# Layer 1 of a four-layer transformer on one core: FFN products issued ahead of the gates, SiLU written as a sigmoid, gate products on GpSimd, norms and copies on two engines

## The chip, the cores and the metric

The kernel runs on 1 core of a Trainium2 chip. A core has five engines that run side by side, each with an instruction queue of its own, in order: TensorE (PE; its weight loads are shown apart as PEld), VectorE (DVE), ScalarE (ACT), GpSimd (POOL) and SyncE (SP), which here issues nearly all ordinary DMAs. Data lies in SBUF (128 partitions); matmul results go to PSUM, which has 8 banks of 128 x 512 floats here. Engines wait for each other by semaphores. The metric is device time in microseconds; lower is better. All data is float32.

## What is computed

A stream `x` of 4 x 512 tokens of 128 features passes four layers. Each layer is a half-weighted FFN, an attention (or a recurrence) and the same FFN again, each on a normalised copy of `x`:

```python
x = x + 0.5 * ffn(layernorm(x));  x = x + attn(layernorm(x));  x = x + 0.5 * ffn(layernorm(x))
```

The layers that matter here are 1 and 2. The FFN of layer 1 has 8 experts of width 64 and a shared expert of width 128. Each token is given the two experts with the largest scores:

```python
shared = (silu(x @ ws_gate.T) * (x @ ws_up.T)) @ ws_down.T
scores = sigmoid(x @ gate_weight.T)              # 8 per token
topk_w, topk_idx = top_k(scores, 2)
topk_w = topk_w / (sum(topk_w) + 1e-20) * 2.5    # combine: these, on the two experts, else 0
hmid = silu(x @ w_gate.T) * (x @ w_up.T)         # per expert, 64 wide
out = sum_over_experts(combine * (hmid @ w_down.T)) + shared
```

`silu(g)` is `g * sigmoid(g)`. The FFN of layer 2 has no nonlinearity between its two matrices, so the kernel multiplies them beforehand into one 128 x 128 matrix per expert; its two gates are a softmax over two scores, worked out as sigmoids of their difference. The "attention" of layer 2 is a gate, `sigmoid(a) * silu(b)`, a scan along the sequence with decay 0.9, and an output matrix. Layers 0 and 3 have causal attention of 16 heads and FFNs that send tokens to experts.

## The kernel before, in words

**Tiling.** The stream stays in SBUF as four tiles `xs[b]` (b = 0 to 3), each 512 tokens as 4 blocks of 128 rows by 128 features. Layers 1 and 2 work on *pairs*: the first pair is b = 0, 1, the second b = 2, 3. The code is written as Python generators; `skewed` (L1437) runs one part of each in turn, with the second pair some rounds behind: 5 rounds in the first FFN of layer 1 (L1504) and 8 in the long chain (L1536).

**Order.** The order of each engine's instructions is set by the framework's planner, which goes by the written order and by its own estimate of when inputs are ready. In the attentions the order of PE, DVE, ACT and POOL is as written (L804). In the long chain, POOL's order alone is as written (L1535).

**Stages.** In order of time: layer 0; `prep_l2` (L1214), the products of layer 2's matrices, beside the end of layer 0's second FFN; the first FFN of layer 1 (`l1_ffn`, L1075); layer 1's attention (`l1_attn`, L1143); then the chain (`behind`, L1508), which is for each pair: layer 1's second FFN, layer 2's FFN (`l2_ffn`, L1254), its recurrence (`l2_attn`, L1323), its second FFN, and the sending of tokens to layer 3's experts (L408, indirect DMAs on POOL); then layer 3.

**A norm.** `norms` (L152): DVE works out mean and variance of each block of 128 tokens (L160, L161); POOL makes `rs`, `rstd` and `off` for all blocks (L164 to L169); then each block is scaled by rstd and shifted, by the engine that the caller names (L171 to L178). `normed_T` (L1039) asks for ACT, turns the blocks on PE (`T_f`, L187) and copies them out of PSUM on ACT (`nT`, L1046). It has five callers' runs per pair: `l1_ffn` twice, `l2_ffn` twice, `l2_attn` once.

**The FFN of layer 1.** The scores are matmuls of 8 columns (`scored`, L1051), then a sigmoid on ACT (L1081). The gates are 16 small DVE instructions (`route` twice, `without`, L1083 to L1094). They are turned on PE (`gT`, L1068), copied by ACT (L1070), written to DRAM and read back spread over 64 partitions per expert (`cb`, L1102), on SP's queue. Then, for each b of the pair, five steps: the shared expert first (k = 0), then two experts at a time (k = 1 to 4). A step is

```python
nc.tensor.matmul(ps[0], gw, nTs[x], start=True, stop=True)     # L1127
nc.tensor.matmul(ps[1], uw, nTs[x], start=True, stop=True)     # L1128
nc.scalar.activation(h, ps[0], AF.Silu)                        # L1130
nc.vector.tensor_tensor(h, h, ps[1], ALU.mult)                 # L1131
nc.vector.tensor_tensor(h, h, cbs[x][:, c, :], ALU.mult)       # L1133, k > 0 only
```

and two steps later its down product (L1115, accumulated in one PSUM bank). At the end of each b the bank is added to `xs[b]` (L1140). `h` has 6 buffers.

**Other names.** `copy` (L131) takes DVE and ACT in turn, by a count over the whole program. In `prep_l2`, for each of 8 experts, PE turns one matrix, ACT copies it (L1246), PE multiplies (L1249), and ACT copies the result into `m` (L1252). L1267 and L1269 are the sigmoids of layer 2's gates, L1333 and L1335 those of the recurrence.

Of the kernel before, what the change touches and what calls it, by code (L numbers as in the profile page):

```python
# [9 lines left out]
FP = mybir.dt.float32  # L10
I32 = mybir.dt.int32
AF = mybir.ActivationFunctionType
ALU = mybir.AluOpType
# [28 lines left out]
def kernel(ctx: ExitStack, tc: tile.TileContext, a: dict, out: bass.AP):  # L42
# [109 lines left out]
    def norms(srcs, dsts, tag, on="vector", fine=False):  # L152

        g = len(srcs) * NT
        st = small.tile([P, g, 6], FP, name=f"st_{tag}", tag=f"bn_st{g}")
        mv = small.tile([P, g, 2], FP, name=f"mv_{tag}", tag=f"bn_mv{g}")
        rs = small.tile([P, g], FP, name=f"rs_{tag}", tag=f"bn_rs{g}")
        rstd = small.tile([P, g], FP, name=f"rstd_{tag}", tag=f"bn_rstd{g}")
        for t in range(g):
            nc.vector.bn_stats(st[:, t, :], srcs[t // NT][:, t % NT, :])  # L160
            nc.vector.bn_aggr(mv[:, t, :], st[:, t, :])  # L161
            if fine and t % 2 and t < g - 1:
                yield
        nc.gpsimd.tensor_scalar(rs, mv[:, :, 1], EPS, None, ALU.add)  # L164
        nc.gpsimd.tensor_tensor(rstd, rs, mhalf[:, :g], ALU.pow)
        if on != "vector":
            off = small.tile([P, g], FP, name=f"off_{tag}", tag=f"bn_off{g}")
            nc.gpsimd.tensor_scalar(off, mv[:, :, 0], -1.0, None, ALU.mult)
            nc.gpsimd.tensor_tensor(off, off, rstd, ALU.mult)  # L169
        yield  # L170
        for t in range(g):  # L171
            src, dst = srcs[t // NT][:, t % NT, :], dsts[t // NT][:, t % NT, :]
            if on == "scalar":
                nc.scalar.activation(dst, src, AF.Identity, bias=off[:, t : t + 1], scale=rstd[:, t : t + 1])
# [864 lines left out]
    def normed_T(pool, bs, tag):  # L1039

        ns = [work.tile([P, NT, D], FP, name=f"n{b}_{tag}", tag="n", bufs=3) for b in bs]
        yield from norms([xs[b] for b in bs], ns, tag, "scalar")
        nTs = []
        for n, b in zip(ns, bs):
            nT = work.tile([P, S], FP, name=f"nT{b}_{tag}", tag="nT", bufs=4)
            nc.scalar.copy(nT, transposed(n, f"{b}_{tag}"))  # L1046
            nTs.append(nT)
        yield
        return nTs
# [25 lines left out]
    def l1_ffn(pool, i, bs):  # L1075
        tag = f"f1{i}_{bs[0]}"
        G = len(bs) * NT
        nTs = yield from normed_T(pool, bs, tag)
        plg = scored(nTs, l1["gate"], tag)
        sc = pool.tile([P, G, E], FP, name=f"sc_{tag}", tag="sc1")  # L1080
        nc.scalar.activation(sc, plg, AF.Sigmoid)  # L1081
# [12 lines left out]
        nc.vector.tensor_tensor(comb, comb, bc(total, [P, G, E]), ALU.mult)  # L1094
        yield
        cbs = []
        for x, b in enumerate(bs):
            rows = to_rows(pool, comb, x, f"{b}_{tag}")

            cb = pool.tile([P, NC, S], FP, name=f"cb{b}_{tag}", tag="spread", bufs=4)  # L1100
            for u in range(2):
                nc.sync.dma_start(  # L1102
                    cb[u * I1 : (u + 1) * I1],
                    bass.AP(tensor=rows.tensor, offset=rows.offset + u * S, ap=[[0, I1], [2 * S, NC], [1, S]]),
                )
            cbs.append(cb)
        order = [NC] + list(range(NC))
        for x, b in enumerate(bs):
            po = bank(f"o{b}_{tag}").rearrange("p (t d) -> p t d", d=D)
            hs = []  # L1110

            def down(k):

                for t in range(NT):
                    nc.tensor.matmul(  # L1115
                        po[:, t, :],
                        hs[k][:, t * P : (t + 1) * P],
                        l1["down"][order[k]],
                        start=(k == 0 and t == 0),
                        stop=(k == NC and t == NT - 1),  # L1120
                    )

            for k, c in enumerate(order):
                gw = l1["wg"][:, c * P : (c + 1) * P] if c < NC else l1["sg"]
                uw = l1["wu"][:, c * P : (c + 1) * P] if c < NC else l1["su"]
                ps = pair(f"gu{c}_{b}_{tag}")
                nc.tensor.matmul(ps[0], gw, nTs[x], start=True, stop=True)  # L1127
                nc.tensor.matmul(ps[1], uw, nTs[x], start=True, stop=True)  # L1128
                h = pool.tile([P, S], FP, name=f"h{c}_{b}_{tag}", tag="h1", bufs=6)
                nc.scalar.activation(h, ps[0], AF.Silu)  # L1130
                nc.vector.tensor_tensor(h, h, ps[1], ALU.mult)  # L1131
                if c < NC:
                    nc.vector.tensor_tensor(h, h, cbs[x][:, c, :], ALU.mult)  # L1133
                hs.append(h)
# [79 lines left out]
    def prep_l2(pool):  # L1214
# [25 lines left out]
        for e in range(E):  # L1240
# [2 lines left out]
            for c in range(NC):  # L1243
                nc.tensor.transpose(ps[:, c * P : (c + 1) * P], wo[:, c * P : (c + 1) * P], ident)
            woT = pool.tile([P, FF], FP, name=f"wo2T_{e}", tag="woT", bufs=3)
            nc.scalar.copy(woT, ps)  # L1246
            pm = bank(f"m2_{e}")
            for c in range(NC):
                nc.tensor.matmul(  # L1249
                    pm[:, :D], wi[:, c, :], woT[:, c * P : (c + 1) * P], start=(c == 0), stop=(c == NC - 1)  # L1250
                )
            nc.scalar.copy(m[:, e, :], pm[:, :D])  # L1252

    def l2_ffn(pool, i, bs):  # L1254
        tag = f"f2{i}_{bs[0]}"
# [326 lines left out]
```

## Time and profile before

| | us |
|---|---|
| median of 9 runs | 1517.73 (1515.79 to 1520.4) |
| the profiled execution | 1517.43 |
| its span | 1515.5 |
| PE, DVE, ACT, POOL busy | 1266.8, 852.1, 713.1, 654.2 |
| `prep_l2`'s products | about 414 to 438 of the span |
| first FFN of layer 1, from its scores to the last down product | 438.6 to 505.9 |
| layer 1's attention | about 506 to 748 |
| the chain | about 748 to 1012 |

The span is the time from the first to the last instruction of the profiled execution, and stretches are given in microseconds from its start. In a timeline line stand start and length, the engine, the line of the code, the operation, `output<-inputs`, shapes, and in brackets how long the engine had been idle before and what ended that ("issue" where the profile shows nothing). Names are shortened: `h_f`, `cb_f`, `gT_f`, `n_f` are tiles of FFNs, with `_a` those of attentions and of the recurrence. A matmul in float32 is shown as two passes, so the "x" counts of PE are twice those of the code. The granted clock is the share of full speed that the throttle gave to TensorE.

### The profile page before, as it was taken

To read this page: it belongs to the slowest core of one execution; us is meant where nothing else is said; L and a number is where in the kernel's file an instruction comes from. 1 tells how busy PE (TensorE), PEld (TensorE's weight loads), DVE (VectorE), ACT (ScalarE), POOL (GpSimd) and SP (SyncE) were. 2 spreads that over 40 slices of the span, in tenths; PEclk is the share of its full clock that TensorE was granted. 3 is DMA by queue.
4 is the path that set the end of the run, shared out by engine and by line. 5 is a ranking of instruction groups with operands and counts; after the bars stand their busy time and mean duration, and the time that the engine had idled before them with its cause. 6 is when DMAs were issued, how large, how long until landed. Compare 5 with 4: busy or idle time off the path is not lost. (4 is left out here: it accounts for less than half of the span.)

```text
span 1515.5 us, 28724 instructions
## 1 busy us (share of the span) xinstructions
PE 1266.8 (84%) x10645; PEld 812.9 (54%) x10645; DVE 852.1 (56%) x2832; ACT 713.1 (47%) x1487; POOL 654.2 (43%) x776
## 2 busy tenths in 40 slices
PE   4788999996969689999799878729689999998394
PEld 3465666764746366667666656527433333342272
DVE  5226777663335367857556545534377787773342
ACT  1235877871453266867643232103336555564041
POOL 4356768761510287868401111544630234203253
PEclk9898999996999799999999868759889999999597
DMA  8420240002424575331050000032104000000233
GB/s 251 114 58 15 79 173 9 9 18 76 141 59 87 151 232 161 106 120 58 2 107 7 1 0 1 29 85 77 58 20 169 15 11 5 15 2 15 78 85 104
DMA packets 100659, 106.20 MB, mean 70 GB/s; under 512 B 9084, under 2 KB 73832, under 8 KB 100520
## 3 DMA queue, kind: packets, MB, share of 16 engines
q1 hardware_dynamic: 93864, 91.16, 21.0%
q0 software_dynamic: 6656, 13.22, 2.7%
q8 instruction: 84, 1.38, 0.4%
q14 instruction: 55, 0.45, 0.1%
HBM read 62.49 MB, written 41.85 MB: 69 GB/s over the span
## 5 line engine op out<-in xcount | busy, mean ns | idle before, releaser
L632 POOL TENSOR_SCALAR sc_a<-sc_a,top_a 128x128 f32<-128x128 f32 (+3 forms) x256 | 274.9, 1090 | 78.2 <-DVE top_a L617 51.7
L600 PE MATMUL s_a<-k_a,q_a 32*128 32x512 f32 (+3 forms) x1536 | 262.3, 546 | 20.6 <-DMA k_a<-fac_a 13.9
L709 ACT ACTIVATE w_a<-t_a 128x512 f32<-128x512 f32 x256 | 140.1, 595 | 117.2 <-PE t_a L600 89.2
L645 PE MATMUL t_a<-ident,sc_a 128*128 128x128 f32 x1280 | 171.6, 280 | 6.6 <-DVE top_a L621 6.0
L502 POOL DMA_INDIRECT res_f<-y_f,back_f x112 | 110.1, 983 | 134.7 <-ACT y_f L501 101.4
L600 PE MATMUL t_a<-ql_a,k_a 32*128 32x512 f32 x512 | 167.2, 647 | 0.3 <-DVE low_a__12648 L689 0.2
L645 PEld LDWEIGHTS t_a<-ident,sc_a 128*128 128x128 f32 x1280 | 142.5, 143 | 43.2 <-issue 16.1
L634 ACT ACTIVATE sc_a<-sc_a,top_a 128x128 f32<-128x128 f32 (+3 forms) x256 | 135.3, 576 | 28.0 <-DVE top_a L621 27.5
L600 PEld LDWEIGHTS s_a<-k_a,q_a 32*128 32x128 f32 x1536 | 90.8, 187 | 92.1 <-issue 40.3
L654 ACT ACTIVATE w_a<-t_a 128x256 f32<-128x256 f32 (+2 forms) x192 | 94.1, 526 | 67.1 <-PE t_a L645 66.7
L408 POOL DMA_INDIRECT disp_f<-n_f,to_f x96 | 95.1, 990 | 54.8 <-issue 36.7
L514 PE MATMUL o_f<-w_l,h_f 128*128 128x128 f32 (+1 forms) x896 | 113.2, 279 | 3.8 <-DVE o_f L496 3.3
L514 PEld LDWEIGHTS o_f<-w_l,h_f 128*128 128x128 f32 (+1 forms) x896 | 103.1, 184 | 15.0 <-DVE o_f L496 6.0
L479 PE MATMUL h_f<-dT_f,w_l 128*128 128x320 f32 (+1 forms) x256 | 105.6, 549 | 2.8 <-ACT dT_f L457 2.8
L164 POOL TENSOR_SCALAR rs_f<-mv_f 128x4 f32<-128x4 f32 (+1 forms) x23 | 5.8, 250 | 221.2 <-DVE mv_f L161 220.8
L667 PE MATMUL acc_a<-w_a,vpad 128*32 128x128 f32 x2560 | 97.3, 278 | 0.6 <-ACT w_a L654 0.6
L689 DVE TENSOR_REDUCE low_a__12648<-s_a 128x1 f32<-128x512 f32 x128 | 82.0, 684 | 27.8 <-PE t_a L600 20.0
L656 ACT COPY w_a<-t_a 128x256 f32<-128x256 f32 (+2 forms) x192 | 93.5, 526 | 6.2 <-PE t_a L645 6.1
L689 DVE TENSOR_REDUCE low_a__12646<-s_a 128x1 f32<-128x512 f32 x128 | 81.3, 683 | 18.4 <-PE t_a L600 12.5
L621 DVE CUSTOM_DVE_ANT_0 sc_a<-s_a,future 128x128 f32<-128x128 f32 (+3 forms) x128 | 62.3, 486 | 48.8 <-PE s_a L600 40.9
L501 ACT ACTIVATE y_f<-o_f,d_f 128x128 f32<-128x128 f32 (+1 forms) x112 | 38.8, 394 | 106.2 <-DVE o_f L496 102.6
L621 DVE CUSTOM_DVE_ANT_0 sc_a<-s_a,table 128x128 f32<-128x128 f32 (+3 forms) x128 | 62.3, 487 | 42.1 <-PE s_a L600 38.0
(343 smaller groups left out, 2253.7 us busy)
## 6 DMA issues: line engine op xcount, KB each, us to landing
fac_a<-fac_a_sb SPq DMA_DIRECT2D x36, 256.0 KB
disp_f<-zeros_f SPq DMA_DIRECT2D x4, 2080.0 KB
d_f<-disp_f SPq DMA_DIRECT2D x32, 260.0 KB
w_l<-in_L_ffn_w_dram SPq DMA_DIRECT2D x16, 512.0 KB
cb_f<-rows_f SPq DMA_DIRECT2D x16, 512.0 KB
q_a<-fac_a SPq DMA_DIRECT2D x32, 256.0 KB
k_a<-fac_a SPq DMA_DIRECT2D x32, 256.0 KB
r_f<-res_f SPq DMA_DIRECT2D x24, 256.0 KB
```

What stands on the lines that cost most here:

```text
L408: nc.gpsimd.indirect_dma_start(out=self.to[c][i0 + t][:, :], out_offset=bass.IndirectOffsetOnAxis(ap=to[:, c, t : t + 1], axis=0), in_=ns[ ...
L479: nc.tensor.matmul(ps[u][:, :cap], w1[:, e, (c + u) * P : (c + u + 1) * P], dT, start=True, stop=True)
L502: nc.gpsimd.indirect_dma_start(out=self.back[e * per + s][:, :], out_offset=bass.IndirectOffsetOnAxis(ap=back[:m, s : s + 1], axis=0), in_ ...
L514: nc.tensor.matmul(po[:m, s, :], h[:, c, s * P : s * P + m], w2[:, e, c, :], start=(c == 0), stop=(c == NC - 1),)
L600: nc.tensor.matmul(ps[:, n0:n1], q[r : r + SLOT, i * P : (i + 1) * P], k[r : r + SLOT, n0:n1], start=True, stop=True)
L621: nc.vector.tensor_tensor_reduce(sc, banks[r][:, :n], more, -1.0, HUGE, ALU.add, ALU.min, top)
L632: nc.gpsimd.tensor_scalar(sc, sc, top, None, ALU.subtract)
L634: nc.scalar.activation(sc, sc, AF.Exp, bias=top, scale=-1.0)
L645: nc.tensor.transpose(ps[:, x * n + j * P : x * n + (j + 1) * P], st["sc", u, i, r0 + x][:, j * P : (j + 1) * P], ident,)
L667: nc.tensor.matmul(st["acc", u][r * SLOT : (r + 1) * SLOT, i * P : (i + 1) * P], vpads[b % 2][:, j, g * 4 + r, :], st["w", u, i, r][:, j * ...
L689: nc.vector.tensor_reduce(st["low", u][:, i, c : c + 1], ps, AX.X, ALU.max, negate=True)
L709: nc.scalar.activation(w, ps, AF.Exp)
```

## The change

- `norms` gets a way "both": even blocks are scaled on DVE by `tensor_scalar` with mean and rstd, odd blocks on ACT with rstd and `off`. `normed_T` asks for it.
- In `l1_ffn` a step's two products, sigmoid and multiplications are a function `up(x, k)`. For the pair's first b, `up(0, 0)` (the shared expert) is written behind the scores' sigmoid and ahead of the gates, and `up(0, 1)` behind the gates and ahead of their transposes. The others stay in their loop.
- `h` is made by a sigmoid on ACT and two multiplications on DVE, by `ps[0]` and by `ps[1]`.
- The multiplication by the gates (`cb`) is on POOL.
- `prep_l2` uses `copy` for its 16 copies.
- Behind `prep_l2`, one sigmoid of a single column of `m`, whose result nothing reads, is written on ACT.

```diff
@@ norms
-            if on == "scalar":
+            if on == "scalar" or (on == "both" and t % 2):
                 nc.scalar.activation(dst, src, AF.Identity, bias=off[:, t : t + 1], scale=rstd[:, t : t + 1])
@@ normed_T
-        yield from norms([xs[b] for b in bs], ns, tag, "scalar")
+        yield from norms([xs[b] for b in bs], ns, tag, "both")
@@ l1_ffn
-        plg = scored(nTs, l1["gate"], tag)
         sc = pool.tile([P, G, E], FP, name=f"sc_{tag}", tag="sc1")
-        nc.scalar.activation(sc, plg, AF.Sigmoid)
+        nc.scalar.activation(sc, scored(nTs, l1["gate"], tag), AF.Sigmoid)
+        order = [NC] + list(range(NC))
+        hs = {}
+
+        def up(x, k):
+            c = order[k]
+            gw = l1["wg"][:, c * P : (c + 1) * P] if c < NC else l1["sg"]
+            uw = l1["wu"][:, c * P : (c + 1) * P] if c < NC else l1["su"]
+            ps = pair(f"gu{c}_{bs[x]}_{tag}")
+            nc.tensor.matmul(ps[0], gw, nTs[x], start=True, stop=True)
+            nc.tensor.matmul(ps[1], uw, nTs[x], start=True, stop=True)
+            h = pool.tile([P, S], FP, name=f"h{c}_{bs[x]}_{tag}", tag="h1", bufs=6)
+            nc.scalar.activation(h, ps[0], AF.Sigmoid)
+            nc.vector.tensor_tensor(h, h, ps[0], ALU.mult)
+            nc.vector.tensor_tensor(h, h, ps[1], ALU.mult)
+            hs[x, k] = h
+
+        up(0, 0)
         yield
...
         nc.vector.tensor_tensor(comb, comb, bc(total, [P, G, E]), ALU.mult)
+        up(0, 1)
         yield
...
             for k, c in enumerate(order):
-                nc.tensor.matmul(ps[0], gw, nTs[x], start=True, stop=True)
-                nc.tensor.matmul(ps[1], uw, nTs[x], start=True, stop=True)
-                nc.scalar.activation(h, ps[0], AF.Silu)
-                nc.vector.tensor_tensor(h, h, ps[1], ALU.mult)
+                if (x, k) not in hs:
+                    up(x, k)
                 if c < NC:
-                    nc.vector.tensor_tensor(h, h, cbs[x][:, c, :], ALU.mult)
+                    nc.gpsimd.tensor_tensor(hs[x, k], hs[x, k], cbs[x][:, c, :], ALU.mult)
@@ prep_l2
-            nc.scalar.copy(woT, ps)
+            copy(woT, ps)
...
-            nc.scalar.copy(m[:, e, :], pm[:, :D])
+            copy(m[:, e, :], pm[:, :D])
@@ after prep_l2
+        first = small.tile([P, 1], FP, name="first_sigmoid", tag="first_sigmoid", bufs=1)
+        nc.scalar.activation(first, l2["m"][:, 0, 0:1], AF.Sigmoid)
```

More of the change, by code (lines that the diff above doesn't have):

```diff
@@ L1106, in l1_ffn @@
             cbs.append(cb)
-        order = [NC] + list(range(NC))
         for x, b in enumerate(bs):
             po = bank(f"o{b}_{tag}").rearrange("p (t d) -> p t d", d=D)
-            hs = []
             def down(k):
@@ L1116, in down @@
                         po[:, t, :],
-                        hs[k][:, t * P : (t + 1) * P],
+                        hs[x, k][:, t * P : (t + 1) * P],
                         l1["down"][order[k]],
@@ L1123, in l1_ffn @@
             for k, c in enumerate(order):
-                gw = l1["wg"][:, c * P : (c + 1) * P] if c < NC else l1["sg"]
-                uw = l1["wu"][:, c * P : (c + 1) * P] if c < NC else l1["su"]
-                ps = pair(f"gu{c}_{b}_{tag}")
-                nc.tensor.matmul(ps[0], gw, nTs[x], start=True, stop=True)
-                nc.tensor.matmul(ps[1], uw, nTs[x], start=True, stop=True)
-                h = pool.tile([P, S], FP, name=f"h{c}_{b}_{tag}", tag="h1", bufs=6)
-                nc.scalar.activation(h, ps[0], AF.Silu)
-                nc.vector.tensor_tensor(h, h, ps[1], ALU.mult)
+                if (x, k) not in hs:
+                    up(x, k)
                 if c < NC:
-                    nc.vector.tensor_tensor(h, h, cbs[x][:, c, :], ALU.mult)
-                hs.append(h)
+                    nc.gpsimd.tensor_tensor(hs[x, k], hs[x, k], cbs[x][:, c, :], ALU.mult)
                 if k > 1:
```

## The prediction

> **What bounds the kernel now.** I read the page first (span, busy times), then the busy table by stretch, then the timeline of the stretches that the change touches, then groups of instructions by shape. The page:
>
> ```profile
> span 1515.5 us, 28724 instructions
> PE 1266.8 (84%) x10645; PEld 812.9 (54%) x10645; DVE 852.1 (56%) x2832; ACT 713.1 (47%) x1487; POOL 654.2 (43%) x776
> ```
>
> TensorE (PE) bounds the whole, but a change off it only pays where PE waits. The table by stretch (stretch, length, busy time of PE, PEld, DVE, ACT, POOL, granted clock, DMA share, GB/s):
>
> ```profile
> 440.50:446.00 5.50, 0.16 (x2) 0.12 (x2) 3.22 (x17) 3.81 (x8) 0.00 (x0) 0.68 0.00 0
> 466.00:506.00 40.00, 40.00 (x190) 25.56 (x188) 21.70 (x38) 10.01 (x17) 2.56 (x4) 1.00 0.25 54
> 752.00:757.00 5.00, 0.00 (x0) 0.00 (x1) 3.40 (x19) 3.35 (x8) 2.42 (x4) 0.61 0.00 0
> 757.00:802.00 45.00, 44.49 (x212) 28.65 (x212) 23.03 (x60) 17.52 (x29) 2.76 (x4) 0.97 0.46 96
> 883.00:912.00 29.00, 20.23 (x64) 12.03 (x64) 10.52 (x47) 12.21 (x28) 7.17 (x10) 0.59 0.00 1
> ```
>
> In both runs of the layer-1 FFN PE is full once products flow (40.00 of 40.00), and empty while the gates of the first pair are worked out; the clock then falls to 0.68 and 0.61. In the later chain (883 to 912) PE waits and runs at 0.59. The timeline at the two gate gaps (start, length, engine):
>
> ```profile
> 440.63 1.28 ACT L1081 ACT_TABLE_LOAD   x1 [1.20 <-issue]
> 442.23 0.22 DVE L218 TENSOR_REDUCE mx<-sc_f 128x8 f32<-128x64 f32 x1 [10.09 <-ACT sc_f L1081]
> 445.90 1.86 PE L1068 MATMUL gT_f<-ident,comb_f 128*8 128x128 f32 x8 [5.34 <-issue]
> ...
> 752.27 0.25 POOL L164 TENSOR_SCALAR rs_f<-mv_f 128x8 f32<-128x8 f32 x1 [1.17 <-DVE mv_f L161]
> 757.03 1.86 PE L1068 MATMUL gT_f<-ident,comb_f 128*8 128x128 f32 x8 [5.37 <-issue]
> 760.20 2.58 SPq L1102 DMA_DIRECT2D cb_f<-rows_f  x4
> 798.35 0.64 POOL L164 TENSOR_SCALAR rs_f<-mv_f 128x8 f32<-128x8 f32 x1 [43.42 <-DVE mv_f L161]
> ```
>
> PE idles 5.34 and 5.37 us behind table load, gates on DVE and their transposes. Further on, ACT applies norms while PE waits:
>
> ```profile
> 849.71 1.26 ACT L174 ACTIVATE n_a<-x,off_a,rstd_a 128x128 f32<-128x128 f32 x3 [8.75 <-POOL off_a L169]
> 850.99 1.28 ACT L1267 ACT_TABLE_LOAD   x1
> 852.50 2.02 ACT L174 ACTIVATE n_a<-x,off_a,rstd_a 128x128 f32<-128x128 f32 x5
> 887.57 3.20 ACT L174 ACTIVATE n_a<-x,off_a,rstd_a 128x128 f32<-128x128 f32 x8 [13.15 <-POOL off_a L169]
> 890.67 3.17 ACT L174 ACTIVATE n_f<-x,off_f,rstd_f 128x128 f32<-128x128 f32 x8
> ```
>
> **Part by part.** Minus is faster, in us.
>
> *Table loads.* Eleven loads of 1.283 stand at L1081, L1130 and L1267. With sigmoid alone, one stays at the start of the chain (attention's exponentials stand before it), and one moves to the early dummy, beside ACT's idle time after 419; if the planner puts it late, the 1.28 returns. Only two of the nine that vanish are on the path: 440.63 (in the gap below) and 850.99 (in the norms below); the rest lie beside a full PE. The Trainium skill ("ScalarE: Activation LUTs", What ACT_TABLE_LOAD costs) gives about 2.66 for a switch, drain included. Here the activation follows 0.01 after the 1.283 load, so the rows disagree; by the page the two would be worth 5.3 where the rows give 2.6.
>
> *Products in front of the gates, first FFN.* A step of two products is 4 matmul passes spaced 0.43 = 1.72, so two steps bring 3.44 of PE work into the gap. The gap loses the load (1.28), and gains what DVE does for those steps inside the gates: four multiplications of 0.687 at most, 2.76; none at least. I take 0.7, one of them, since the first sigmoid ends late in the 3.6 of gate work. Left idle: 5.34-1.28+0.7-3.44 = 1.3, gain 4.0 (2.0 to 4.7). The passes behind the gap run at 0.85 instead of 0.43, about 1.7 lost up to 449.7; a gap of 1.3 spares part: 1.0 (0 to 1.7). The second pair's gates leave PE idle 464.3 to 465.6, which its own early products fill: 1.0 (0 to 1.3).
>
> *The same in the chain.* Here the load stays: gain 3.44-0.7 = 2.7 (0.7 to 3.4), clock 1.0 (0 to 1.8).
>
> *Silu by sigmoid, gates' products on POOL.* ACT's instruction stays 0.60. DVE gets one more multiplication a step and loses one in four steps of five: 1.37 in a PE step of 2.61 (1.72 and 0.88 for the down product): hidden. On POOL the product takes, by the nearest row of the same form, L1200, 1.277 where L1133 took 0.688 on DVE, and it is behind the extra multiplication. So a step is 0.69+0.59 = 1.3 later; down products lag two steps, so PE covers it except at the end of the first FFN, where the last down product had some 0.1 to 0.3 to spare: +1.0. Ends: +0.6, and +2.3 if POOL's product doubles to 2.55, as L632's 128x512 scalar form (1.569) does against L1428's (0.773). The Trainium skill ("GPSIMD Engine Reference", 4.1 Engine selection) speaks against this move: two-input work belongs on VectorE, GpSimd being about 2x slower. By the rule's price alone 32 products cost 32x0.6 = 19 more; by the rows nearly all of it is beside PE.
>
> *POOL's queue in the chain.* There POOL runs in written order. The second pair's norm (POOL at 752.27 now) is written after the first pair's products 1 to 3, and those need cb. Its load is issued at 760.20; the first DVE product with it runs at 767.98, 10.9 after the gates' transposes. After: 767.9+3x1.28 = 771.8, norm ops 2.65, applied by 776.4; its gates at about 784.5 (782.9 now), its cb at 795.5. Four products (three of the second pair, the first pair's last) then stand before the first pair's next norm: that one is applied at about 805.4, its transposes now at 806.1. Behind the waiting POOL stand the norms, then PE's transposes. PE has in these waits the other half's steps, up to the six h buffers; I count 2.0 of new idle (0 if all is filled; 10 if both waits, about 11 each less some 6 of own work, stay open: +10). The old stall at 801.8 (2.47, DVE waiting for ACT behind the norm) and the slow clock after it (1.8) mostly go: -2.0 (0 to -4.3).
>
> *Norms on two engines.* Eight of 0.40 on ACT become four there (1.65) beside four on DVE (L178: 0.31 to 0.82; about 0.28 each when queued, 1.1). DVE's need only rstd, 0.6 before off. Where PE waits this counts: l2_attn at 849.7, 1.6 and the load's 1.28 and 0.6 of PE at the slow clock, -3.5 (2 to 4.5); at 887.6 two norms in a row, 6.3 to about 3.3, -3.0 (2 to 4). At 832.3 and 922.9 PE is full and it is 0; if that cover went, each would give 1.6. Inside attention the first pair's move is 4x0.35 of DVE for 4x0.40 of ACT: 0 (-0.5 to 0.5).
>
> *Copies of the layer-2 product on two engines.* copy() alternates, and 38 calls precede these, so all eight 128x512 copies fall to DVE (0.69 for 0.586) and the small ones stay on ACT (0.27). PE waits on each big one: +0.1x8 = +0.8, and DVE's statistics at 425 to 432 are mixed in. Against this ACT no longer holds copies behind norms (PE waits 2.83 for one at 433.85), and the norm is split. Together -1.0 (0 to -2).
>
> Sum: first FFN -1.0-4.0-1.0-1.0+1.0 = -6.0; chain -2.7-1.0+2.0-2.0 = -3.7; norms -6.5. Total -16.2. No DMA is added; SP's four loads keep their order. Behind the chain everything waits for the last dispatch, so the shift passes on. The profiled execution took 1517.43 (span 1515.5), 0.3 below the median 1517.73: 1501 after.
>
> **Rivals.** *A, the queue bites:* both cb waits stay open, +8 on my +2, and only half of -6.0 comes: about -5, 1512. For it: 43.42 of POOL idle now, all free; against: PE has the other half's work. *B, slower:* POOL's queue again, with products doubled to 2.55: the seven that stand before the two norms add 7x1.28 = 9 to the open waits' 10, PE's clock falls in each wait (1.7 each, as behind 445.9), and the first FFN's end costs 2.3. That is 1517.4-16.2-2.0+22.4+1.3 = 1522.9; it decides once the queue costs more than 16.9. Against: L977, L1200 and L1419, same form, never pass 1.294 beside a busy DVE. *C, it doesn't do what it says:* the planner puts the gates' transposes first on PE, so the gaps stay: lost are 4.0-1.28 (the load goes anyway), 1.0, 1.0, 2.7, 1.0 = 8.4: 1510. For it: now PE had ready products and did not take them at 440.6; against: they are now written ahead.
>
> **How the numbers follow.** Forecast 0.62, A 0.14, B 0.10, C 0.14. What a measurement can tell from no change is 0.2%, 3 us. Slower: B and a little, 0.10. Same: A's upper edge, 0.05. Faster: 0.85. Range: all good ends, first FFN -2.0-4.7-1.7-1.3+0.6 = -9.1, chain -3.4-1.8-4.3 = -9.5, norms -8.5, sum -27, give 1490; upward A and C must be in, 1514. The forecast's own range is 1493 to 1508.
>
> **What would show it.** Right: one sigmoid load at the chain's start, none in the FFNs; PE's gap behind the scores under 3 us and the granted clock there over 0.8; norms in halves of four on ACT and DVE; transposes at the l2_attn norms 3 us closer to their statistics. Wrong: the second pair's POOL norm more than 26 us behind the first pair's gate transposes; POOL products over 1.5; PE idle over 3 us behind cb.

## The result and the profile after

The changed kernel takes 1528.69 us (median of 10, 1527.01 to 1530.33), the kernel before in the same series 1518.53: a ratio of 1.0067 (1.0058 to 1.0076), 10.2 us slower. Forecast were 1501 and a range of 1490 to 1514. The profiled execution took 1530.27, its span is 13.1 longer than before. First the page:

```profile
span 1528.6 us, 28753 instructions
PE 1271.7 (83%) x10645; PEld 814.5 (53%) x10645; DVE 878.5 (57%) x2888; ACT 681.7 (45%) x1431; POOL 693.2 (45%) x808
```

ACT lost 31 of its work, DVE gained 26 and POOL 39. PE has 5 more for the same 10645 passes: parts of them ran at a slower clock, as the stretches show. The table by stretch (columns as in the prediction), for the stretches that answer to those shown of before:

```profile
440.50:453.00 12.50, 8.88 (x25) 4.94 (x26) 5.69 (x21) 2.91 (x7) 0.00 (x0) 0.68 0.01 1
474.00:510.00 36.00, 35.19 (x165) 22.17 (x164) 21.11 (x39) 8.45 (x15) 17.21 (x15) 1.00 0.28 60
755.00:764.00 9.00, 4.58 (x19) 2.34 (x18) 5.70 (x24) 2.59 (x4) 0.18 (x1) 0.92 0.00 0
764.00:820.00 56.00, 46.81 (x206) 30.95 (x205) 29.32 (x69) 14.56 (x28) 20.01 (x20) 0.89 0.36 77
899.00:926.00 27.00, 17.50 (x64) 10.68 (x64) 14.60 (x56) 9.23 (x20) 7.48 (x10) 0.68 0.00 1
```

Once products flow in the first FFN, PE is still full (35.19 of 36.00). Two stretches got worse. In front of the first transposes of the gates there were 5.5 us of a nearly empty PE; now there are 12.5, with 8.88 of work at a clock of 0.68. And the second FFN, where PE had 44.49 of 45.00, now has 46.81 of 56.00: 9.2 idle, in waits of 2.39, 1.98, 1.50, 2.03 and 1.30.

**The first gap**, in the timeline of the changed kernel:

```profile
439.39 0.49 ACT L174 ACTIVATE n_f<-x,off_f,rstd_f 128x128 f32<-128x128 f32 x1 [2.07 <-POOL off_f L169]
440.41 1.06 PE L1055 MATMUL lg_f<-gate1T,nT_f 128*128 128x8 f32 x8 [2.52 <-ACT nT_f L1046]
444.85 0.22 DVE L218 TENSOR_REDUCE mx<-sc_f 128x8 f32<-128x64 f32 x1 [0.45 <-ACT sc_f L1080]
446.50 0.69 DVE L1095 TENSOR_TENSOR h_f<-h_f,gu_f 128x512 f32<-128x512 f32 x1 [1.43 <-PE gu_f L1090]
448.84 0.69 DVE L1094 TENSOR_TENSOR h_f<-h_f,gu_f 128x512 f32<-128x512 f32 x1 [1.25 <-ACT h_f L1093]
449.63 0.69 DVE L1095 TENSOR_TENSOR h_f<-h_f,gu_f 128x512 f32<-128x512 f32 x1
452.55 0.23 DVE L1112 TENSOR_TENSOR comb_f<-comb_f,total_f 128x64 f32<-128x64 f32 x1
452.88 1.01 PE L1068 MATMUL gT_f<-ident,comb_f 128*8 128x128 f32 x4 [3.62 <-issue]
```

DVE's queue holds the early steps' multiplications (L1094, L1095) between the gates' instructions. They cost more than their 0.69: the queue is in order, so it stood 1.43 for PE and 1.25 for ACT, with ready gate instructions behind. The gates (17 instructions on DVE in the trace) take 7.9 (444.85 to 452.78) instead of 3.6 (442.23 to 445.80). They also begin later: an ACT norm of the second pair (439.39) stands ahead of the first pair's copies, PE waits 2.52 for those (0.35 before), and the first early product runs between the two halves of the scores. The transposes come at 452.88 instead of 445.90.

**POOL's queue in the chain**, again of the changed kernel:

```profile
763.55 1.86 PE L1068 MATMUL gT_f<-ident,comb_f 128*8 128x128 f32 x8 [4.42 <-issue]
766.71 2.58 SPq L1121 DMA_DIRECT2D cb_f<-rows_f  x4
774.54 3.71 POOL L1144 TENSOR_TENSOR h_f<-h_f,cb_f 128x512 f32<-128x512 f32 x3 [19.36 <-DMA cb_f<-rows_f]
775.85 4.57 PE L1132 MATMUL o_f<-wd1T,h_f 128*128 128x128 f32 x24 [2.39 <-POOL h_f L1144]
778.33 0.25 POOL L164 TENSOR_SCALAR rs_f<-mv_f 128x8 f32<-128x8 f32 x1
782.40 1.56 PE L1132 MATMUL o_f<-wd1T,h_f 128*128 128x128 f32 x8 [1.98 <-POOL h_f L1144]
783.75 1.92 PE L187 MATMUL T_f<-ident,n_f 128*128 128x128 f32 x8
809.91 4.98 POOL L1144 TENSOR_TENSOR h_f<-h_f,cb_f 128x512 f32<-128x512 f32 x4 [4.63 <-DMA cb_f<-rows_f]
815.71 0.24 POOL L164 TENSOR_SCALAR rs_f<-mv_f 128x8 f32<-128x8 f32 x1 [0.82 <-DVE mv_f L161]
818.13 0.33 PE L187 MATMUL T_f<-ident,n_f 128*128 128x128 f32 x1 [2.03 <-DVE n_f L178]
```

The second pair's norm (778.33) stands behind three products that waited for `cb`; it was at 752.27, ahead of the first pair's gates. Its transposes, at 768.78 before, are at 783.75. The first pair's next norm (815.71) comes behind four more: the first pair's last product, which its residual needs, stands in POOL's queue behind one that waited for the second pair's `cb` until 809.91. The products themselves take 1.28 in the mean. (In the prediction's count the norm was to be applied by 776.4; the gates and so `cb` came later, the order is the one foreseen.)

**A gain that did not arrive.** The first norm of the recurrence is applied as forecast:

```profile
866.61 1.65 ACT L174 ACTIVATE n_a<-x,off_a,rstd_a 128x128 f32<-128x128 f32 x4 [8.98 <-POOL off_a L169]
867.56 2.49 POOL L977 TENSOR_TENSOR x<-x,bout 128x512 f32<-128x512 f32 x2 [0.99 <-DVE apart_f L1275]
867.96 0.95 DVE L226 TENSOR_TENSOR mask<-eq,first 128x64 f32<-128x64 f32 x1
868.87 1.27 DVE L1284 TENSOR_TENSOR mask<-mask,g_f 128x64 f32<-128x64 f32 x1
870.68 1.97 PE L1294 MATMUL gT_f<-ident,gates 128*128 128x128 f32 x8 [1.77 <-DVE gates L1288]
872.44 3.24 PE L1341 MATMUL proj_a<-nT_a,win 128*128 128x512 f32 x4
```

From POOL's `rs` to the end of ACT's norm it took 7.43 (847.09 to 854.52), now 4.50 (863.76 to 868.26): 2.9 won. But to the first `proj` (L1331 before, L1341 now) it took 9.83 and now takes 8.68. In PE's order the other pair's gates (L1294) stand ahead of `proj`, and they are late: two of their DVE instructions, 0.22 elsewhere, take 0.95 and 1.27 beside POOL's addition of L977. (In the kernel before this addition fell beside their last two instructions, at 852.99: 1.40 for both instead of 0.31.)

The lengths of stretches, from single lines of the traces. "First FFN" is from `T_f` to its last residual, "to gates" from the attention's last residual to the first pair's transposes, "to norm" from there to POOL's `rs` of that pair's next norm, "rest" from there to the first dispatch:

| kernel | first FFN | to gates | to norm | rest |
|---|---|---|---|---|
| before | 68.7 | 8.4 | 41.3 | 158.0 |
| changed | 74.8 | 11.0 | 52.2 | 153.6 |
| difference | +6.1 | +2.6 | +10.9 | -4.4 |

That is +15.2; the attention between was 1.8 shorter (it lies between 240.2 and 243.7 in all traces here, whatever the kernel).

### The profile page after: what moved, and what is told of

Its sections match the earlier page's. It is cut to its first block, busy times and chain, and to the rows that moved or that the text cites. A ratio compares the mean times of both kernels' runs of the same rounds, so it can differ in the third digit from the quotient of the medians.

```text
span 1528.6 us, 28753 instructions
## 1 busy us (share of the span) xinstructions
PE 1271.7 (83%) x10645; PEld 814.5 (53%) x10645; DVE 878.5 (57%) x2888; ACT 681.7 (45%) x1431; POOL 693.2 (45%) x808
## 5 line engine op out<-in xcount | busy, mean ns | idle before, releaser
L645 PEld LDWEIGHTS t_a<-ident,sc_a 128*128 128x128 f32 x1280 | 141.9, 142 | 42.6 <-issue 16.0
L514 PEld LDWEIGHTS o_f<-w_l,h_f 128*128 128x128 f32 (+1 forms) x896 | 103.1, 184 | 14.8 <-DVE o_f L496 6.0
L689 DVE TENSOR_REDUCE low_a__12688<-s_a 128x1 f32<-128x512 f32 x128 | 81.3, 683 | 18.1 <-PE t_a L600 12.2
L1144 POOL TENSOR_TENSOR h_f<-h_f,cb_f 128x512 f32<-128x512 f32 x32 | 40.4, 1276 | 102.6 <-DVE h_f L1095 54.1
```

The lines of the kernel that those rows point to most:

```text
L514: nc.tensor.matmul(po[:m, s, :], h[:, c, s * P : s * P + m], w2[:, e, c, :], start=(c == 0), stop=(c == NC - 1),)
L645: nc.tensor.transpose(ps[:, x * n + j * P : x * n + (j + 1) * P], st["sc", u, i, r0 + x][:, j * P : (j + 1) * P], ident,)
L689: nc.vector.tensor_reduce(st["low", u][:, i, c : c + 1], ps, AX.X, ALU.max, negate=True)
```

## Experiments

They were made on several chips; the kernel before took 1518.9 on the first (e1 to e4) and 1536 on the others. So kernels are compared by their ratio to the kernel before in the same series, and 0.1% is 1.5 us. The stretches of all traces can stand side by side even so: what the other chips take longer lies for the most part behind them (from the first dispatch to the end 557.7 to 559.3 in the traces of before, changed and e1 to e4, 571.7 to 578.0 in the others). But each is read from one trace, and the kernel before has none on those chips. Kernels with the same code in the first FFN differ there by up to 2.3 (e4 72.4, e9 72.6, e15 74.7), so a smaller difference of a stretch shows nothing. The theories: **Q**, POOL's queue in the chain; **G**, the gates stretched by multiplications. L numbers are those of the changed kernel; in rows of e10, e13 and e15 they are of their own code, where L1127 and L1128 (e10) or L1092 and L1093 (e13) are a step's products, L1070 the transposes of the gates in e13, L1122 the gates' last instruction, L1098 and L1099 the multiplications, and L1156 POOL's product in e15.

**e1, the gates' products on DVE again**

```diff
-                    nc.gpsimd.tensor_tensor(hs[x, k], hs[x, k], cbs[x][:, c, :], ALU.mult)
+                    nc.vector.tensor_tensor(hs[x, k], hs[x, k], cbs[x][:, c, :], ALU.mult)
```

> The changed kernel with one thing undone: the multiplication by the gates (32 of them) is on DVE again. Theory Q (POOL's written order: the second pair's norm, and then the first pair's next norm, stand behind products that wait for cb): both waits go, the second pair's norm on POOL is back ahead of the first pair's gates (about 756 instead of 778.3), the first pair's next norm 10 or 11 us earlier than its 815.7, and the end 0.8 of the first FFN too: 1516 to 1519 where the changed kernel has 1528.7. Theory G (gates stretched on DVE by the early steps' multiplications): that part stays, and the queue was only late because the gates were: only the 0.8 to 2 at the ends of the FFNs come back, 1526 to 1528. By either, the gates' transposes stay near 452.9 in the first FFN.

Measured: 0.9997 (0.9985 to 1.0008). The stretch to the norm is 41.2, the first FFN still 74.7. In time all of the loss comes back, as Q has it; but two losses and two gains of the change may cancel, so the others follow.

**e2, without the early steps**

```diff
-        up(0, 0)
...
-        up(0, 1)
```

> The changed kernel without the products ahead of the gates: all ten steps of a pair are in their loop, everything else as changed. Theory G: the gates' 16 small instructions run without multiplications between them again, the transposes in the first FFN are at 447 to 449 instead of 452.9 and in the chain 2.6 closer to the attention's end, but PE is idle for some 3 to 4 in the gap: if G is all of it, 1519; if the filled gap is worth as much as the stretch costs, 1528.7 as it is. Theory Q: the order on POOL stays, the two waits for cb stay open, and the time falls by no more than the 3 to 6 of the two stretches: 1523 to 1526.

Measured: 1.0049 (1.0032 to 1.0067). The stretch to the norm stays at 52.5, to the gates it is 8.4 as before, the first FFN 72.8. Q's number. In the changed kernel the early steps thus bring nothing; the 0.18% that they seem to cost lies within the intervals.

**e3, the second pair's norm written ahead of the products**

```diff
-    def skewed(gens, lag):
+    def skewed(gens, lag, early=None):
...
+                if early is not None and i and (r == early or r == i * lag):
+                    if r == early:
+                        next(live[i])
+                    continue
                 if r >= i * lag and next(live[i], "end") == "end":
...
-                whole(skewed([behind(pool, bs) for bs in pairs], 8))
+                whole(skewed([behind(pool, bs) for bs in pairs], 8, 5))
```

> The changed kernel with the second pair's first norm of the chain written ahead of the first pair's products (its first part is taken in round 5 instead of 8), so that on POOL its four instructions stand in front of the products that wait for cb; the products stay on POOL, and the first pair's next norm still stands behind the second pair's products. Theory Q: the second pair's transposes come at 767 to 772 instead of 783.8 and PE's idle time between 760 and 790 (about 9) mostly goes; with the second wait still there, 5 to 8 come back: 1521 to 1524. If the queue is not the cause, or the second wait alone sets the time: 1527 to 1529.

Measured: 1.0026 (1.0015 to 1.0037), 0.41% or 6.2 less than the changed kernel. POOL's rows, and the row of the table by stretch from the first pair's transposes to its next norm:

```profile
760.63 0.25 POOL L164 TENSOR_SCALAR rs_f<-mv_f 128x8 f32<-128x8 f32 x1 [1.17 <-DVE mv_f L161]
780.30 4.95 POOL L1144 TENSOR_TENSOR h_f<-h_f,cb_f 128x512 f32<-128x512 f32 x4 [16.96 <-DMA cb_f<-rows_f]
812.15 0.24 POOL L164 TENSOR_SCALAR rs_f<-mv_f 128x8 f32<-128x8 f32 x1 [1.35 <-DVE mv_f L161]
```

```profile
769.50:812.20 42.70, 42.06 (x202) 27.14 (x203) 24.50 (x61) 11.26 (x20) 13.77 (x12) 0.94 0.47 101
```

POOL waits for `cb` as long as ever, and it costs nothing: PE has 42.06 of 42.70, and the stretch to the norm is 42.6. What cost was the norm behind the wait. In this stretch the first wait is nearly the whole of Q (9.6 of the 10.9); in time e3 brings back 6.2 where e1 brings 10.7.

**e4, the early steps' multiplications behind the gates**

```diff
-            nc.vector.tensor_tensor(h, h, ps[0], ALU.mult)
-            nc.vector.tensor_tensor(h, h, ps[1], ALU.mult)
+            def times():
+                nc.vector.tensor_tensor(h, h, ps[0], ALU.mult)
+                nc.vector.tensor_tensor(h, h, ps[1], ALU.mult)
...
+            if gated:
+                with tc.issue_after(gated[0]):
+                    times()
+            else:
+                held.append(times)
...
-        nc.vector.tensor_tensor(comb, comb, bc(total, [P, G, E]), ALU.mult)
         up(0, 1)
+        gated.append(nc.vector.tensor_tensor(comb, comb, bc(total, [P, G, E]), ALU.mult).ins)
+        for times in held:
+            with tc.issue_after(gated[0]):
+                times()
```

`gated[0]` is the last instruction of the gates on DVE; `issue_after` queues what is written under it behind that instruction.

> The changed kernel with the early products and their sigmoids where they are, but their multiplications on DVE queued behind the last instruction of the gates. Theory G: the gates are worked out in 3.6 instead of 7.7, so the transposes come at about 449 instead of 452.9 in the first FFN and 2.6 earlier in the chain, PE is kept busy by the early products meanwhile, and 4 to 6 come back: 1523 to 1525. If the multiplications between the gates are hidden: 1528 to 1529. By theory Q the two waits in the chain stay, so it does not reach 1518.

Measured: 1.0051 (1.0035 to 1.0067), 0.16% less, which lies within the intervals and between the two sides. The gates run in 3.6 again and their transposes come 12.2 after `T_f` instead of 16.0; but the first FFN is still 72.4.

**e5, e1 and e4 together**

> The changed kernel with the gates' products on DVE again and the early steps' multiplications behind the gates. Theory Q and G together: what the two changes brought alone (10.2 and 2.1) adds up, the stretch from the attention's end to the first pair's gate transposes is 8.9 as before, the first pair's next norm comes 41 us after them, and what the split norms give behind the second FFN (about 4) is left over: 1513 to 1517. Rival (the multiplications and the products both load DVE, so they get in each other's way once all are there): 1518 to 1521.

Measured: 0.9937 (0.9916 to 0.9959): more than the sum of e1 (0.70% below the changed kernel) and e4 (0.16%), more also than the theory had, and faster than the kernel before. First FFN 66.5, to the gates 9.5, to the norm 38.9, rest 152.5. So, by these traces, each of the two faults hid the other's price in the first FFN (74.8 to 74.7 by e1, to 72.4 by e4, to 66.5 by both).

**e6, the kernel before with the split norms alone** (`norms` and `normed_T` as in the change)

> The kernel before with one part of the change alone: the norms of normed_T applied by DVE and ACT in turn. Theory: the 3.9 that the changed kernel is shorter from the second pair's residual to the last dispatch is this part's (my prediction gave it 6.5), less up to 1.5 in the first FFN, where the second pair's ACT half gets ahead of the first pair's copies: 1513.5 to 1516. Rival: those 3.9 come from the table loads that went, and then this one stays at 1517 to 1519.

Measured: 0.9988 (0.9972 to 1.0003), -1.8 or nothing. Rest 155.0 (3.0 less), first FFN 70.7, to the gates 10.4: what the norms win in the recurrence, this trace loses again in front of layer 1's gates.

**e7, the kernel before with the products on POOL alone** (its L1133 on `nc.gpsimd`)

> The kernel before with one part of the change alone: the multiplication by the gates on POOL, silu and the rest as before. Theory Q: the queue needs nothing else: the second pair's norm stands behind the products that wait for cb, the stretch from the first pair's gate transposes to its next norm is 52 instead of 41.3, and with 1 to 2 at the end of the first FFN the time is 1528 to 1531. Rival (the queue only costs because the early products made cb late): 1519 to 1522.

Measured: 1.0033 (1.0016 to 1.0050), +5.1, between the two sides (the theory had 9.5 to 12.5 more than the kernel before, the rival 0.5 to 3.5). The second pair's norm is 14.7 behind the gates' transposes and the stretch to the norm is 49.4, so the queue stretches this part without the rest of the change; but the rest is 152.7, 5 less than before without any norm split. How the two pairs stand to each other changes that stretch too, and the 4.4 won there in the changed kernel are therefore not the norms' alone.

**e8, e5 with layer 1's FFN norms on ACT and the first early product behind the scores on PE**

```diff
-        nTs = yield from normed_T(pool, bs, tag)
+        nTs = yield from normed_T(pool, bs, tag, "scalar")
...
-        up(0, 0)
+        with tc.issue_after(last[0]):
+            up(0, 0)
```

`last[0]` is the last matmul of the scores.

> As e5 (products on DVE, multiplications of the early steps behind the gates), and besides: the FFN norms of layer 1 on ACT alone as before, so that DVE has no norm in front of the gates, and the first early product behind all the scores' matmuls on PE. Theory G: the first FFN gets 3 to 4 shorter than in e5 (transposes 9 to 10 after T_f instead of 12.2, PE warm), the chain's start 0 to 1: 1510 to 1513. Rival (the start of the first FFN is set by ACT's copies and not by these): as e5 within 1, 1513 to 1517.

Measured: 0.9909 (0.9890 to 0.9927), the fastest: 14 less than the kernel before. First FFN 66.2, to the gates 8.4, to the norm 38.9. The 3 to 4 that the theory expected in the first FFN did not come (66.5 in e5; the transposes are 12.0 behind `T_f`, not 9 to 10), and the 0.28% below e5 is no more than the intervals leave open.

**e9, e3 and e4 together (products on POOL)**

> The changed kernel with the products still on POOL, but with both cures at once: the second pair's first norm of the chain written ahead of them, and the early multiplications behind the gates. Theory: queue (-6.2 alone) and gates (-2.1 alone) are separate losses and add up: 8 less than the changed kernel, a ratio to the kernel before of 0.999 to 1.003. What it then still lies above the version with the products on DVE (ratio 0.9937) is the price of a POOL product itself: its 1.27 instead of 0.69, the two-input instructions of DVE that take 1.25 instead of 0.22 beside it, and the first pair's next norm that still stands behind the second pair's products. Rival (POOL's products cost nothing but the first wait): 0.994 to 0.996.

Measured: 0.9997 (0.9985 to 1.0010). In the chain it equals e5 (9.5, 39.4, 152.6); in the first FFN it has 72.6 against 66.5.

**e10, the kernel before with silu by a sigmoid alone**

```diff
-                nc.scalar.activation(h, ps[0], AF.Silu)
+                nc.scalar.activation(h, ps[0], AF.Sigmoid)
+                nc.vector.tensor_tensor(h, h, ps[0], ALU.mult)
...
+        first = small.tile([P, 1], FP, name="first_sigmoid", tag="first_sigmoid", bufs=1)
+        nc.scalar.activation(first, l2["m"][:, 0, 0:1], AF.Sigmoid)
```

> The kernel before with one part of the change alone: silu as a sigmoid and a second multiplication on DVE, and the early sigmoid that loads the table; products where they were, gates' products on DVE. Theory: of the nine loads that go, two are on the path, 1.28 in front of the first pair's gates in the first FFN and up to 1.28 in the norm of the recurrence; the 40 added multiplications of 0.69 lie beside PE except between the second pair's gates: 1 to 3 faster, a ratio of 0.998 to 0.9995. Rival (the multiplications delay the second pair's gates, where DVE has them in its queue with the steps): 1.001 to 1.003.

Measured: 1.0035 (1.0018 to 1.0052), 5.4 slower, the rival's side. From its timeline and its table by stretch:

```profile
476.06 1.86 PE L1068 MATMUL gT_f<-ident,comb_f 128*8 128x128 f32 x8 [2.84 <-DVE mv_a L161]
477.72 1.91 PE L1127 MATMUL gu_f<-nT_f,sg1T 128*128 128x512 f32 x2
```

```profile
470.00:482.00 12.00, 8.77 (x38) 5.40 (x37) 8.28 (x34) 1.75 (x3) 2.54 (x3) 0.72 0.11 33
```

The first pair's gates do gain the table load (7.4 from `T_f` to the transposes, 8.7 before). The second pair's lose it: among them DVE now has two multiplications a step, the transposes come 22.3 after the first pair's instead of 19.7, PE waits 2.84 and comes back at a slow clock. (The row names the last DVE instruction ahead of it; the gates' own ended at 475.91.) Before, the same wait was 1.33 and the eight passes behind it took 1.03. The slow clock does not follow from the wait alone: in e12 the same wait is 2.84 too and the clock stays. In the chain the second pair's transposes come 27.7 after the first pair's instead of 25.9, and the stretch to the norm is 45.0, 3.7 more; but the rest is 154.6, 3.4 less. So in this trace the loss lies in the first FFN (73.2, 4.5 more); how the measured 5.4 divides is not shown.

**e11, the kernel before with the copies of `prep_l2` by `copy` alone**

> The kernel before with one part of the change alone: the copies of layer 2's products by DVE and ACT in turn. Theory: the loop that PE waits on ends 0.4 earlier, as in the changed kernel (T_f at 436.85 instead of 437.22), and nothing behind it changes: a ratio of 0.999 to 1.0005. Rival (the prediction's 1.0 and more): 0.998 to 0.999.

Measured: 1.0008 (0.9996 to 1.0020): nothing. (The first FFN of its trace is 71.6 even so, 2.9 more than before.)

**e12, e8 without the early steps**

> The best version so far (ratio 0.9909: products on DVE, layer 1's FFN norms on ACT, early steps with late multiplications) without the early steps. Theory: the early steps are worth what the prediction gave them where the gates stay whole, 4.0 and 1.0 in the first FFN and 2.7 and 1.0 in the chain: this one loses 6 to 9 of the 14, a ratio of 0.9950 to 0.997. Rival (the gap is filled, but cb ends as late as before, so down products wait instead): 0.991 to 0.993.

Measured: 1.0014 (1.0000 to 1.0028): the early steps are worth 1.05%, 16, in e8: more than the theory's 6 to 9. First FFN 72.5 against 66.2, to the norm 46.2 against 38.9. The second pair's late gates of e10 are here again (22.1 behind the first pair's, PE waits 2.84), and in e8 the second pair's own early steps fill that wait.

**e13, the kernel before with the early steps alone** (as in e8; silu, one multiplication a step, copies and norms as before)

> The kernel before with the early steps alone, in the good form (behind the scores on PE, their multiplication behind the gates on DVE): silu with its table loads, the gates' products on DVE, norms and copies on ACT as before. Theory: what the early steps bring does not need the sigmoid: PE's gaps of 5.3 in front of the first pair's transposes are filled, and the second pair's early steps stand ready when its gates are late, so that PE stays warm there: 8 to 14 faster, a ratio of 0.991 to 0.995. Rival (the table loads, sigmoid for the scores and silu for the early steps in turn on ACT, eat the gain): 0.996 to 1.000.

Measured: 0.9917 (0.9894 to 0.9940). Of its timeline:

```profile
450.81 1.92 PE L1092 MATMUL gu_f<-nT_f,wg1T 128*128 128x512 f32 x2
452.52 1.24 PE L1093 MATMUL gu_f<-nT_f,wu1T 128*128 128x512 f32 x2
453.59 1.04 PE L1070 MATMUL gT_f<-ident,comb_f 128*8 128x128 f32 x8
466.64 0.71 PE L1070 MATMUL gT_f<-ident,comb_f 128*8 128x128 f32 x5
```

PE reaches both pairs' transposes without a wait and at full speed. First FFN 65.1, to the norm 37.8. Within the intervals this one part is as fast as e8: the other parts of the change that e8 keeps add nothing to it.

**e14, the changed kernel with products on DVE and without the early steps** (e1 and e2 together)

> The changed kernel with its gates' products on DVE and without the early steps: beside the changed kernel with its products on DVE (ratio 0.9997) it shows what the early steps bring in the form they were made in, with their multiplications between the gates. Theory: the multiplications take back what the filled gap brings, because the transposes come 3 to 4 later: the early steps are worth 0 to 3 in this form against 16 in the good one, a ratio of 0.9995 to 1.002. Rival (worth nearly the whole even so, and the rest of the change costs it): 1.005 to 1.010.

Measured: 1.0030 (1.0014 to 1.0046). Beside e1 (0.9997) the early steps in the form they were made in are worth 0.33%, 5: between theory and rival, a third of their worth in e8.

**e15, e5 with the first FFN's products on POOL**

```diff
+                    (nc.gpsimd if i == 0 else nc.vector).tensor_tensor(hs[x, k], hs[x, k], cbs[x][:, c, :], ALU.mult)
```

> The version with products on DVE and late multiplications (ratio 0.9937), but with the products of the first FFN on POOL, where POOL's order is the planner's and nothing of the chain is touched. Theory: of the 9 that POOL's products cost once queue and gates are mended, 6 lie in the first FFN: the second pair's gates are worked out beside POOL's products, where the two-input instructions of DVE take up to 1.25 instead of 0.22, and half of its transposes stand on PE behind down products that wait for POOL; the first FFN takes 72 to 73 instead of 66.5 and the ratio is 0.997 to 0.999. Rival (POOL's products cost in the chain only): 0.993 to 0.995.

Measured: 0.9997 (0.9980 to 1.0014), 0.60% above e5, a little past the theory's side: the whole remainder that e9 showed lies in the first FFN (74.7). Its timeline at the second pair's gates:

```profile
465.06 3.74 POOL L1156 TENSOR_TENSOR h_f<-h_f,cb_f 128x512 f32<-128x512 f32 x3 [20.36 <-DVE mx L218]
465.18 1.27 DVE L221 TENSOR_TENSOR eq<-eq,e_rank 128x64 f32<-128x64 f32 x1
467.77 1.12 DVE L226 TENSOR_TENSOR mask<-eq,first 128x64 f32<-128x64 f32 x1
470.36 1.26 POOL L1156 TENSOR_TENSOR h_f<-h_f,cb_f 128x512 f32<-128x512 f32 x1 [1.55 <-DVE h_f L1099]
470.45 1.25 DVE L1122 TENSOR_TENSOR comb_f<-comb_f,total_f 128x64 f32<-128x64 f32 x1
471.76 1.23 PE L1068 MATMUL gT_f<-ident,comb_f 128*8 128x128 f32 x5 [4.15 <-DVE comb_f L1122]
478.52 0.49 PE L1068 MATMUL gT_f<-ident,comb_f 128*8 128x128 f32 x3
```

A two-input 128x64 instruction of DVE that begins while a POOL product runs lasts until that is done, and PE waits 4.15 for the transposes; in e5 it is 0.15:

```profile
467.58 1.04 PE L1068 MATMUL gT_f<-ident,comb_f 128*8 128x128 f32 x8 [0.15 <-DVE comb_f L1122]
```

The planner also put products of the `down` step, which wait for POOL, between the transposes (471.76 and 478.52), so the second half of `cb` is asked for 7 later. How the 9 divide between these two was not taken apart.

## Why the prediction was wrong

By its own steps, the sizes in us:

| step | forecast | shown |
|---|---|---|
| POOL's queue in the chain | +2.0 | +10.9 in the stretch; -6.2 when the norm alone is moved ahead (e3) |
| DVE's early multiplications inside the gates | 0.7 of at most 2.76 | gates 4.4 longer; taken out, -2.4 alone (e4, within the intervals), -9.2 beside e1 (e5) |
| second multiplication | 0, hidden | +5.4 alone, table loads gained (e10) |
| gates' products on POOL, first FFN | +1.0 | up to 9 beside whole gates (e15) |
| early steps, all terms | -9.7 | -12.7 with the multiplications behind the gates (e13); as made, -5 (e1 beside e14) or nothing clear (e2) |
| norms | -6.5 | -1.8 (-4.3 to +0.5) (e6) |
| copies and norms ahead of the first FFN | -1.0 | copies +1.2 (-0.6 to +3.1) (e11) |

All but the early steps add up when taken alone: e6, e7, e10 and e11 give +9.9, and e2, which has the four together, +7.4, equal within their intervals.

- **The queue.** The step foresaw the place exactly: the second pair's norm 14.8 behind the transposes (771.8 less 757.0), and 14.8 it is. What failed is "PE has in these waits the other half's steps ... I count 2.0 of new idle". The other half is what the norm holds back: without it PE has only the first pair's steps, whose down products wait for the same `cb`. So PE had 9.2 of idle time in the stretch, and of the range given, 0 to 10, the upper end came true. The old stall before the first pair's next norm, which was to go mostly (-2.0), is still there: 2.03 at 818.13 and 1.30 behind it. The sign that the text gave for this step, more than 26 behind, was set too far: 14.8 was already the loss. So was the other, PE idle over 3 behind `cb`: it was 2.39 and 1.98, in two pieces.
- **The gates.** "four multiplications of 0.687 at most, 2.76; none at least. I take 0.7, one of them" bounded the multiplications by their own length. In an in-order queue each also brings its wait for PE or ACT, 2.7 together here, so the upper end was not one. The gap was to be under 3 at a clock over 0.8; it was 3.62, behind 8.9 of work at 0.68. That early steps are worth having was right: 9.7 forecast, 12.7 in e13 (9.2 to 16.3), 16 in e8.
- **The second multiplication.** "1.37 in a PE step of 2.61 (1.72 and 0.88 for the down product): hidden" compared sums over a step. Where the second pair's gates run through the same queue, DVE sets when PE gets its transposes. In e10's trace the first FFN lost 4.5 there, of which 2.7 go with the slow clock behind that wait; the chain as a whole lost nothing.
- **Products on POOL.** Their length was right (1.28 in the mean, never doubled), and so, nearly, was the price at the end of the first FFN: +1.0 forecast, and PE waits 0.79 for the last product. Left out was that they hold up DVE. The rule of the Trainium skill that the prediction weighed ("GPSIMD Engine Reference", 4.1 Engine selection: two-input work belongs on VectorE) was the better guide to the side, but not by the price of a product: the 19 that the prediction set beside it does not show (e7 costs 5.1), and what cost was the queue and DVE held up.
- **Norms.** The first norm of the recurrence was applied as forecast, 2.9 sooner; behind the second, `proj` came 1.7 sooner (from POOL's `rs` 9.43 and now 7.73), where 3.0 was forecast. At the first, the next wait, for the other pair's gates, took back 1.8. In front of layer 1's gates the DVE half delays them (10.4 to the gates in e6, 8.4 before), which the prediction left out.
- **The rivals.** B had the side and the queue, with a price of 1522.9; its doubled products did not occur, and without them the queue, the stretched gates and the second multiplication reached 1528.7. A has the mechanism of the queue (both waits stay open, though in e3 the second costs the stretch next to nothing) and too small a price. C did not occur: the transposes wait for the gates, and early products run ahead of them.
- Right were the table loads: none is left in the FFNs, and the one at the chain's start (755.81) stays.

## What to carry to other kernels

Before work is moved to an engine with a written order, list what stands behind it there and ask what the other engines do while it waits: here one norm behind three waiting products emptied PE, and with the norm in front the same wait cost nothing. Work that fills a gap must not enter the queue that ends the gap: products on PE ahead of the gates were worth 13 with their multiplications behind the gates, and a third of it or less with them inside. An engine with free time on average is not free in the stretch where another waits for its last result.

## What the runs showed of the hardware

- **DVE stands still beside a POOL product.** In the traces with products on POOL, two-input 128x64 instructions of layer 1's gates that begin while a product runs take up to 1.27, just until it ends (465.06 and 465.18 above); in those with the products on DVE (before, e1, e5, e8) none of them passes 0.23. Multiplications with one operand in PSUM keep their 0.69 beside it, and reductions, with one input, their 0.22. The Trainium skill ("SBUF — State Buffer", SBUF: two separate sides) says that DVE and GpSimd share one port pair as an exclusive lock, which a DVE instruction with two SBUF inputs also needs against a GpSimd instruction that reads SBUF, and that the loser waits for the whole instruction. These rows agree, and the rule would have told against products on POOL beside the gates.
- **The length of a wait does not alone settle PE's clock.** In front of the second pair's transposes in the first FFN, PE waits 2.84 both in e10 and in e12. In e10 (its rows above) the eight transposes behind it took 1.86, the next passes 0.95 each instead of 0.43, and the clock in the stretch was 0.72; from the start of the transposes to the fourth product behind them it took 6.11 (476.06 to 482.17). In e12 all of it ran at full speed:

```profile
469.29 1.03 PE L1068 MATMUL gT_f<-ident,comb_f 128*8 128x128 f32 x8 [2.84 <-DVE mv_a L161]
472.74 1.02 PE L1090 MATMUL gu_f<-nT_f,su1T 128*128 128x512 f32 x2
```

The same way took 3.45 there, as behind the wait of 1.33 in the kernel before (3.44, 465.64 to 469.08). So a slow clock behind such a wait cost 2.7 here, and these runs do not show what decides whether it comes. In the first FFN and the chain of all traces, every wait of PE over 3 that began at full clock was followed by a slow one; of those between 1.6 and 3 some were (1.65 in e2, at 792.74) and some not (2.92 in e9, at 765.07).
